# Cross-attention weights transposed by DMA instead of TensorE, in a quantised transformer layer on one core

## The chip, the cores and the metric

The kernel runs on one core of a Trainium2 chip. The metric is device time in microseconds (us). A core has TensorE (PE in the profile; PEld is its weight load), VectorE (DVE), ScalarE (ACT), GpSimd (POOL) and SyncE (SP), which here only issues DMAs. Each engine runs its own instructions in order and waits for the others through semaphores; DMAs move data in the background.

## The reference, cut to what matters

For 32 batches of 100 rows, `x` (32, 100, 256) is normalised and attends to a context of 361 rows with 16 heads of width 64; then comes a feed-forward layer whose operands are quantised.

```python
Qh = einsum('btd,hdk->bhtk', layernorm(x), WQ)
Kh = einsum('btd,hdk->bhtk', ctx, WK)
Vh = einsum('btd,hdv->bhtv', ctx, WV)
logits = einsum('bhtk,bhsk->bhts', Qh, Kh) / 8 + mask * -1e9
attn = softmax(logits)
A = einsum('bhts,bhsv->bhtv', attn, Vh)      # heads side by side
x = x + A @ WO
x = x + qlinear(gelu(qlinear(layernorm(x), W1, b1)), W2, b2)
```

The change concerns `attn`. Scores come out with the 100 query rows on partitions and the 361 context rows in the free dimension; the product with `Vh` sums over context rows, so it needs `attn` with the context rows on partitions. Every one of the 512 matrices (32 batches, 16 heads) of 100x361 float32 has to be transposed.

## The kernel before, in words

Batches are handled one after the other, 16 heads as 8 pairs (`NHP`); a pair's two heads lie in the lower and the upper 64 partitions of queries (`qbuf`) and keys (`kT`). Batch 0 and batch 31 are cut into three steps of 2, 2, 4 and 4, 2, 2 pairs; the other 30 batches are one step each ("whole", `turns` in the code). Four batches make a group: queries, and the product with `WO`, are computed for a group at once.

The main loop (from L616) issues for a whole batch, on PE in just this order, since PE is kept to the order of the source by `manual_schedule` while the other engines are left to a planner:

- For each of the 8 pairs, in turn: `weights_T` (L363) of the batch before: 12 PE transposes (2 heads, 3 chunks of 128 context rows, 2 halves of 50 queries; L373) into two PSUM banks, and two copies to `pT` (L385, on ACT but for the first, which is on DVE); then the scores of the pair (L423), into two PSUM banks. DVE adds the mask, writes the scores to the SBUF buffer `pb` (16 slots, one a head) and finds each row's extreme (L434); ACT then makes the exponentials and their sums (L404), DVE the reciprocals of the sums and the division (L443, L449).
- `attend` of the batch before (L468): `pT` times the values, copied to `aT` by ACT (L475).
- `v_part` (L287), the batch's values, copied by DVE (L294).
- A group's work, in one of the four batches each: `project_T` (`py`, L505), `project_back` (`po`, L519) with the residual on DVE and a store by POOL (L529 to L546, L135), `ln1_T` (`ptx`, L336), `q_part` (`pq`, L348).
- `k_part` of the next batch (`pk`, L256): 8 pairs, copied to `kT` by ACT (L263).

The 50-query halves lie at partitions 0 and 64 (`RH`), so scores take 114 partitions (`TP`). All PSUM tiles of attention share a ring of 8 banks (`bank`, L191), handed out in the order of the source. Contexts are loaded by SP (L197) into three buffers, two or three batches ahead. Steps of quantising the feed-forward weights (`quantize_weight`, L559) are put in two to a batch. The feed-forward part (from L680) follows when attention has ended.

The two functions that do the transposing and hand it on, as they are before:

```python
for h in range(2):
    for c in range(NSC):
        for k in range(2):
            ks = slice(k * RH, k * RH + TH)
            nc.tensor.transpose(
                pts[k][:SC, (h * NSC + c) * TH : (h * NSC + c + 1) * TH],
                pb[ks, h0 + h, c * SC : (c + 1) * SC],
                ident[ks, ks],
            )
```

Of the kernel before, what the change touches and what calls it, by code (L numbers as in the profile page):

```python
# [8 lines left out]
F32 = mybir.dt.float32  # L9
BF16 = mybir.dt.bfloat16  # L10
I16 = mybir.dt.int16
# [10 lines left out]
BIG = 3.4e38  # L22
# [5 lines left out]
def kernel(  # L28
# [34 lines left out]

    TH, RH = T // 2, P // 2
    TP = RH + TH

# [72 lines left out]
    def normalize(b, after, engine=nc.vector):  # L139

        xb = xg[b // G][:, b % G, :]
        i = engine.tensor_scalar(
            xb, xb, mv2[:, b, 0:1], rstd2[:, b : b + 1], ALU.subtract, ALU.mult
        )
        follow(i, after)
# [13 lines left out]
    with ExitStack() as att:  # L159
# [14 lines left out]
        maskt = wpool.tile([TP, S], F32, tag="maskt", name="maskt")  # L174
        nc.gpsimd.memset(maskt, 0.0)
# [3 lines left out]
        pb = wpool.tile([TP, 2 * NHP, SP], F32, tag="p", name="p")  # L179
        for t in cbuf:  # L180
# [4 lines left out]
            wpool.tile([P, PAIRS, G, 2, RH], F32, tag=f"q{q}", name=f"q{q}") for q in range(NQ)  # L185
        ]
        for t in qbuf:
            for j in range(G):
                nc.gpsimd.memset(t[:, :, j, 0, TH:], 0.0)
# [31 lines left out]
        for k in range(2):  # L221
            nc.scalar.dma_start(
                out=maskt[k * RH : k * RH + TH], in_=mask[k * TH : (k + 1) * TH]
            )
        load_w(nc.sync, wqt, 0, wq)
# [16 lines left out]
        steps = []  # L242
        for b in range(B):
            first = 0
            for n in parts.get(b, (NHP,)):
                steps.append((b, first, n))
                first += n
# [93 lines left out]
        def q_part(g, q):  # L341

            if g >= NG:
                return
            for pair in range(PAIRS):
                pq = bank(f"pq{g}_{q}_{pair}")
                for dc in range(NDC):
                    nc.tensor.matmul(  # L348
                        pq[:, :GT],
                        wqt[q][:, dc, pair * P : (pair + 1) * P],  # L350
                        xnTs[g][:, dc, :],
                        start=(dc == 0),
                        stop=(dc == NDC - 1),
                    )
                nc.vector.tensor_scalar(
                    qbuf[q][:, pair, :, :, :TH],
                    pq[:, :GT].rearrange("p (j k t) -> p j k t", j=G, k=2),
                    -1.0 / DK**0.5, None, ALU.mult,
                )
# [3 lines left out]
        def weights_T(i, pair, on_vector):  # L363
# [5 lines left out]
# [3 lines that stand above are left out]
                        ks = slice(k * RH, k * RH + TH)  # L372
                        nc.tensor.transpose(  # L373
                            pts[k][:SC, (h * NSC + c) * TH : (h * NSC + c + 1) * TH],
                            pb[ks, h0 + h, c * SC : (c + 1) * SC],
                            ident[ks, ks],
                        )
            pT = pTs[i, pair] = p1.tile(
                [SC, 2 * NSC, 2, TH], F32, tag=f"pT{pair}", name=f"pT{i}_{pair}"
            )  # L380
            copies = []
            for k in range(2):
                src = pts[k][:SC, : 2 * NSC * TH].rearrange("p (c t) -> p c t", t=TH)
                copy = nc.vector.tensor_copy if k == 0 and on_vector else nc.scalar.copy
                copies.append(copy(pT[:, :, k, :], src))  # L385
            return copies

        def scores(i):

            b, first, n = steps[i]
            g, j = b // G, b % G
            _, p0, before = steps[i - 1] if i else (0, 0, 0)
            turns = n == NHP
            heads = range(2 * first, 2 * (first + n))
            rsum = small.tile([TP, 2 * NHP], F32, tag="rsum", name=f"rsum{i}")
            r = small.tile([TP, 2 * NHP], F32, tag="r", name=f"r{i}")
            ms = {}

            def exponentials(heads):
                for h in heads:
                    s = pb[:, h, :S]
                    done = nc.scalar.activation(  # L404
                        s, s, AF.Exp, bias=ms[h], scale=-1.0, accum_out=rsum[:, h : h + 1]
                    )
                    if turns:
                        follow(done, copied)

            if not turns:  # L410
                for pair in range(p0, p0 + before):
                    weights_T(i - 1, pair, True)
            for pairs in ([q] for q in range(first, first + n)) if turns else (
                range(q, q + PAIRS) for q in range(first, first + n, PAIRS)
            ):
                if turns and pairs[0] < before:
                    copied = weights_T(i - 1, p0 + pairs[0], pairs[0] == 0)[1]
                pss = {}
                four = range(2 * pairs[0], 2 * pairs[-1] + 2)
                for h in four:  # L420
                    pair, k = divmod(h, 2)
                    pss[h] = bank(f"sc{i}_{h}")
                    nc.tensor.matmul(  # L423
                        pss[h][:TP, :S],
                        qbuf[pair // PAIRS][
                            k * DK : (k + 1) * DK, pair % PAIRS, j, :, :
                        ].rearrange("p k t -> p (k t)")[:, :TP],
                        kT[k * DK : (k + 1) * DK, pair, :],
                        start=True,
                        stop=True,  # L430
                    )
                for h in four:
                    ms[h] = small.tile([TP, 1], F32, tag=f"m{h}", name=f"m{i}_{h}", bufs=1)
                    found = nc.vector.tensor_tensor_reduce(  # L434
                        pb[:, h, :S], pss[h][:TP, :S], maskt, 1.0, BIG, ALU.add, ALU.min, ms[h]
                    )
                if not turns:
                    exponentials(four)
            if turns:
                exponentials(heads)  # L440
            at_once = 1 if i == len(steps) - 1 else 4
            for h0 in heads[::at_once]:
                last = nc.vector.reciprocal(  # L443
                    r[:, h0 : h0 + at_once], rsum[:, h0 : h0 + at_once]
                )
                follow(last, found)
                for h in range(h0, h0 + at_once):
                    s = pb[:, h, :S]
                    nc.vector.tensor_scalar(s, s, r[:, h : h + 1], None, ALU.mult)  # L449
            return last  # L450

        def attend(i, pairs=None):
# [8 lines left out]
            for p0 in range(first, first + n, HP):  # L461
                m = min(HP, n)
                av = bank(f"av{i}_{p0}")
                for pair in range(p0, p0 + m):
                    for c in range(NSC):
                        for k in range(2):
# [4 lines left out]
                                pTs[i, pair][:, k * NSC + c, :, :].rearrange("p k t -> p (k t)"),  # L471
# [87 lines left out]
        def quantize_weight(src, rows, dst, name, n, after):  # L559
# [16 lines left out]
            if n == NWP:  # L576
                al = small.tile([P, NWP], F32, tag="aal", name=f"aal{name}")
                nc.gpsimd.partition_all_reduce(al, am, P, bass_isa.ReduceOp.max)
                sw = const.tile([P, 1], F32, tag=f"sw{name}", name=f"sw{name}")
                rw = small.tile([P, 1], F32, tag="rw", name=f"rw{name}")  # L580
                nc.vector.tensor_reduce(sw, al, AX.X, ALU.max)
# [3 lines left out]
            if n > NWP:  # L585
# [3 lines left out]
                nc.vector.tensor_scalar(  # L589
# [9 lines left out]
        for b in range(G):  # L599
            stats1(b)  # L600
        nc.vector.tensor_scalar(maskt, maskt, 1e9, None, ALU.mult)
# [10 lines left out]


        todo = [(w, n) for w in ("1", "2") for n in range(2 * NWP + 1)]
        weights = {"1": (w1T, NDC, w1qt), "2": (w2T, NFC, w2qt)}
        for i, (b, first, n) in enumerate(steps):  # L616
            g, j = b // G, b % G
            begun = [h for h in range(2) if first <= h * HP < first + n]
            ended = [h for h in range(2) if first < (h + 1) * HP <= first + n]
            last = scores(i)  # L620
            if i >= 1:
                attend(i - 1)
# [13 lines left out]
            for h in ended:  # L636
                k = 2 * j + h
                if k < G:
                    stats1((g + 1) * G + k, last)
                if k == 2 * (G - 2) + 1:  # L640
                    ln1(g + 1, first_copied)
                if g >= 1 and 2 <= k < 2 + G:
                    project_back(g - 1, k - 2)
                if k == 2 * (G - 2) + 1:
                    ln1_T(g + 1)
                if j == G - 1:
                    for q in range(2):
                        q_part(g + 1, 2 * h + q)
                if g >= 1 and k == 1:
                    for dc in range(NDC):  # L650
                        project_T(g - 1, dc)
                if h == 1 and b + NCB < B:
                    load_ctx(b + NCB)
# [5 lines left out]
            if i >= 3:  # L659
                for w, p in todo[:2]:  # L660
                    quantize_weight(*weights[w], w, p, last)
                del todo[:2]
# [343 lines left out]
```

## Time and profile before

| what | before |
|---|---|
| median of 3 runs | 1337.61 us (1337.61 to 1337.65) |
| the profiled execution | 1336.85 us |
| its span, first to last instruction | 1335.1 us |
| busy: PE, PEld, DVE, ACT, POOL | 1306.2, 807.5, 774.2, 695.8, 113.6 us |
| instructions: PE, DVE, ACT, POOL | 10062, 2404, 1927, 198 |
| granted TensorE clock | 0.995 |
| DMA | 33.02 MB, mean 25 GB/s |

The span is that of one execution, whose own time is 1.75 us longer. A group row of the profile gives busy time (with overlaps of pipelined instructions counted once) and the mean duration of one instruction; the chain of waits follows the end of the kernel back to its start, each piece once, so its pieces add up.

### The profile page before, as it was taken

To read this page: it belongs to the slowest core of one execution; us is meant where nothing else is said; L and a number is where in the kernel's file an instruction comes from. 1 tells how busy PE (TensorE), PEld (TensorE's weight loads), DVE (VectorE), ACT (ScalarE), POOL (GpSimd) and SP (SyncE) were. 2 spreads that over 40 slices of the span, in tenths; PEclk is the share of its full clock that TensorE was granted. 3 is DMA by queue.
4 is the path that set the end of the run, shared out by engine and by line. 5 is a ranking of instruction groups with operands and counts; after the bars stand their busy time and mean duration, and the time that the engine had idled before them with its cause. 6 is when DMAs were issued, how large, how long until landed. Compare 5 with 4: busy or idle time off the path is not lost.

```text
span 1335.1 us, 25493 instructions
## 1 busy us (share of the span) xinstructions
PE 1306.2 (98%) x10062; PEld 807.5 (60%) x10064; DVE 774.2 (58%) x2404; ACT 695.8 (52%) x1927; POOL 113.6 (9%) x198
## 2 busy tenths in 40 slices
PE   9999999999999999999999999999999999999858
PEld 4666556666566566666566666665666665666426
DVE  4666446664366554664366653664556643576897
ACT  2555345565355455562456453553455543554875
POOL 1000000200011000110011000110001100110260
PEclk9999999999999999999999999999999999999999
DMA  8010001000000000000000000000000000000112
GB/s 247 28 44 13 12 12 44 20 17 1 12 19 18 12 12 1 19 19 12 13 18 19 12 2 12 18 18 12 12 2 18 19 13 12 11 11 4 49 54 99
DMA packets 24864, 33.02 MB, mean 25 GB/s; under 512 B 1828, under 2 KB 22792, under 8 KB 24744
## 3 DMA queue, kind: packets, MB, share of 16 engines
q1 hardware_dynamic: 21776, 24.81, 6.3%
q0 software_dynamic: 2144, 5.38, 1.3%
q8 instruction: 79, 1.29, 0.4%
q10 hardware_dynamic: 824, 1.19, 0.3%
q14 instruction: 41, 0.34, 0.1%
HBM read 24.82 MB, written 6.55 MB: 24 GB/s over the span
## 4 chain that ended last, share of the span: by engine, by line
PE 94%; POOL 2%; issue 2%; ACT 1%; DVE 1%; POOLq 0%; DVEq 0%
PE pv L287 25%; PE pk L256 23%; PE sc L423 13%; PE av L468 10%; PE pt L373 7%; PE pq L348 6%; PE py L505 6%; PE pf L950 2%; PE po L489 1%; ACT h L860 1%; POOL r L797 1%; POOL r L798 1%; PE po L519 0%; PE ptx L336 0%; PE ph L852 0%
## 5 line engine op out<-in xcount | busy, mean ns | idle before, releaser
L287 PE MATMUL pv<-wvt,c 128*128 128x512 f32 x768 | 338.3, 596 | 0.0
L256 PE MATMUL pk<-c,wkt 128*128 128x361 f32 x1016 | 314.2, 467 | 0.0
L263 ACT COPY kT<-pk 128x361 f32<-128x361 f32 x254 | 116.8, 460 | 366.6 <-PE pk L256 366.6
L404 ACT ACTIVATE p<-p,m 114x361 f32<-114x361 f32 x512 | 297.4, 592 | 7.8 <-DVE m L434 7.8
L256 PEld LDWEIGHTS pk<-c,wkt 128*128 128x128 f32 x1016 | 191.9, 190 | 113.2 <-issue 1.0
L434 DVE CUSTOM_DVE_ANT_0 p<-sc,maskt 114x361 f32<-114x361 f32 x512 | 252.2, 533 | 11.9 <-PE sc L423 6.9
L287 PEld LDWEIGHTS pv<-wvt,c 128*128 128x128 f32 x768 | 143.3, 190 | 172.1 <-issue 161.9
L385 DVE COPY pT<-pt 128x300 f32<-128x300 f32 x50 | 22.3, 468 | 351.6 <-PE pt L373 351.6
L423 PE MATMUL sc<-kT,q 64*114 64x361 f32 x1024 | 208.5, 490 | 0.0
L385 ACT COPY pT<-pt 128x300 f32<-128x300 f32 x462 | 168.7, 413 | 74.1 <-PE pt L373 71.4
L373 PEld LDWEIGHTS pt<-ident,p 50*128 50x128 f32 x3072 | 131.1, 139 | 78.1 <-issue 51.5
L449 DVE TENSOR_SCALAR p<-p,r 114x361 f32<-114x361 f32 x512 | 173.5, 403 | 2.6
L294 DVE COPY v<-pv 128x512 f32<-128x512 f32 x192 | 129.4, 680 | 28.6 <-PE pv L287 28.3
L468 PEld LDWEIGHTS av<-pT,v 128*64 128x64 f32 x3072 | 132.8, 137 | 18.5 <-ACT pT L385 15.0
L468 PE MATMUL av<-pT,v 128*64 128x100 f32 x3072 | 140.0, 250 | 0.0
L373 PE MATMUL pt<-ident,p 50*128 50x50 f32 x3072 | 133.5, 221 | 0.3 <-DVE p L449 0.3
L135 POOL TENSOR_TENSOR xb<-x,b2a 100x256 f32<-100x256 f32 x32 | 23.4, 732 | 900.4 <-DVE rmax L529 891.2
L404 ACT ACTIVATION_READ_ACCUMULATOR p<-p,m 114x1 f32 x512 | 99.7, 195 | 0.0
L348 PE MATMUL pq<-xnT,wqt 128*128 128x400 f32 x256 | 87.9, 500 | 0.2 <-ACT xnT L339 0.2
L423 PEld LDWEIGHTS sc<-kT,q 64*114 64x114 f32 x1024 | 76.8, 184 | 4.3 <-issue 0.6
L505 PE MATMUL py<-aT,wot 128*128 128x400 f32 x224 | 76.4, 499 | 0.0
L443 DVE RECIPROCAL r<-rsum 114x4 f32<-114x4 f32 (+1 forms) x131 | 22.8, 175 | 90.2 <-ACT p L404 89.9
(131 smaller groups left out, 730.7 us busy)
## 6 DMA issues: line engine op xcount, KB each, us to landing
c<-in_ctxT_dram SPq DMA_DIRECT2D x31, 361.0 KB, 3.1
x<-in_x_dram SPq DMA_DIRECT2D x8, 400.0 KB
xb<-xb POOLq DMA_DIRECT2D x32, 100.0 KB, 2.1
x<-xb SPq DMA_DIRECT2D x5, 384.0 KB, 3.0
out_dram<-ot SPq DMA_DIRECT2D x3, 384.0 KB, 2.5
wqt<-in_wq_dram SPq DMA_DIRECT2D x4, 256.0 KB
wot<-in_wo_dram SPq DMA_DIRECT2D x1, 1024.0 KB, 8.9
w<-in_w1T_dram POOLq DMA_DIRECT2D x1, 1024.0 KB, 5.4
```

The source lines that it names most:

```text
L256: nc.tensor.matmul(pk[:, :S], wkt[q][:, dc, col * P : (col + 1) * P], c[:, dc, :S], start=(dc == 0), stop=(dc == NDC - 1),)
L287: nc.tensor.matmul(pv[:SC, :], c[:, dc, s * SC : (s + 1) * SC], wvt[h][:, dc, :], start=(dc == 0), stop=(dc == NDC - 1),)
L294: return nc.vector.tensor_copy(vs[b, h][:, s, :], pv[:SC, :])
L348: nc.tensor.matmul(pq[:, :GT], wqt[q][:, dc, pair * P : (pair + 1) * P], xnTs[g][:, dc, :], start=(dc == 0), stop=(dc == NDC - 1),)
L373: nc.tensor.transpose(pts[k][:SC, (h * NSC + c) * TH : (h * NSC + c + 1) * TH], pb[ks, h0 + h, c * SC : (c + 1) * SC], ident[ks, ks],)
L385: copies.append(copy(pT[:, :, k, :], src))
L404: done = nc.scalar.activation(s, s, AF.Exp, bias=ms[h], scale=-1.0, accum_out=rsum[:, h : h + 1])
L423: nc.tensor.matmul(pss[h][:TP, :S], qbuf[pair // PAIRS][k * DK : (k + 1) * DK, pair % PAIRS, j, :, :].rearrange("p k t -> p (k t)")[:, :TP ...
L434: found = nc.vector.tensor_tensor_reduce(pb[:, h, :S], pss[h][:TP, :S], maskt, 1.0, BIG, ALU.add, ALU.min, ms[h])
L449: nc.vector.tensor_scalar(s, s, r[:, h : h + 1], None, ALU.mult)
L468: nc.tensor.matmul(av[k * DK : (k + 1) * DK, (pair - p0) * T : (pair - p0 + 1) * T], vs[b, pair // HP][:, c, h * DK : (h + 1) * DK], pTs[i ...
L505: nc.tensor.matmul(py[:, :GT], wot[:, c, dc * P : (dc + 1) * P], aT[:, c, :, :].rearrange("p j t -> p (j t)"), start=(c == 0), stop=(c == ...
```

## The change

In the 30 whole batches the weights are no longer transposed on PE. The float32 weights are seen as pairs of 16-bit halves. For a pair of heads, POOL copies the 2 x 384 float32 of each query row into one of two buffers `apart`, with the low halves and the high halves of each chunk of 128 in separate rows of 128 (`send`: two copies of 100 x 768 int16). SP then issues one DMA transpose of that buffer (112 x 1536 int16, 336 KB) into one of three buffers `xT`. ACT copies `xT` into `pT`, putting the halves together again (`join`: one copy of 128 x 1200 int16 a pair).

The order of a whole batch is written anew (`whole_batch`), in four quarters of two pairs (four heads): scores of the quarter, then its part of the next batch's keys; `attend` of the batch before in the second quarter; half the values in the third and in the fourth. `pb` has 8 slots instead of 16, so a slot comes round after two quarters. DVE, ACT and POOL, like PE, keep the order of the source within whole batches. Scores of whole batches take 100 partitions instead of 114; the 114-partition mask stays, as `maskh`, for batches 0 and 31, which go on being transposed by PE. Some small work moves (`quantize_weight` in more steps, `load_ctx` to the first quarter of the next batch, the end of a batch's loop body to `rest`).

```diff
+    TR = -(-T // 16) * 16
...
-        pb = wpool.tile([TP, 2 * NHP, SP], F32, tag="p", name="p")
+        NB = 4 * PAIRS
+        pb = wpool.tile([TP, NB, SP], F32, tag="p", name="p")
...
+        apart = [
+            wpool.tile([TR, 2 * NSC * 2 * SC], I16, tag=f"apart{k}", name=f"apart{k}")
+            for k in range(2)
+        ]
...
+        def products(i, pairs):
+            b = steps[i][0]
+            n = TP if halved(b) else T
+            pss = {}
+            for h in range(2 * pairs[0], 2 * pairs[-1] + 2):
+                pair, k = divmod(h, 2)
+                pss[h] = bank(f"sc{i}_{h}")[:n, :S]
+                nc.tensor.matmul(
+                    pss[h],
+                    qbuf[pair // PAIRS][k * DK : (k + 1) * DK, pair % PAIRS, b % G, :n],
+                    kT[k * DK : (k + 1) * DK, pair, :],
+                    start=True,
+                    stop=True,
+                )
+            return pss
+        def minima(i, pss):
+            for h, ps in pss.items():
+                n = ps.shape[0]
+                ms[h] = small.tile([TP, 1], F32, tag=f"m{h}", name=f"m{i}_{h}", bufs=1)
+                done = nc.vector.tensor_tensor_reduce(
+                    pb[:n, h % NB, :S], ps, maskh if halved(steps[i][0]) else maskt, 1.0, BIG,
+                    ALU.add, ALU.min, ms[h][:n],
+                )
+            return done
...
+        xTs, NX = {}, 3
+        def send(i, q):
+            n = NSC * 2 * SC
+            for pair in range(q * PAIRS, (q + 1) * PAIRS):
+                src = apart[pair % 2]
+                for k in range(2):
+                    nc.gpsimd.tensor_copy(
+                        src[:T, k * n : (k + 1) * n].rearrange("t (c l s) -> t c l s", c=NSC, l=2),
+                        pb[:T, (2 * pair + k) % NB, :].bitcast(I16).rearrange(
+                            "t (c s l) -> t c l s", c=NSC, l=2
+                        ),
+                    )
+                xT = xTs[i, pair] = p1.tile(
+                    [SC, 2 * NSC * 2, TR], I16, tag="xT", name=f"xT{i}_{pair}", bufs=NX
+                )
+                nc.sync.dma_start_transpose(out=xT, in_=src)
+        def join(i, q):
+            for pair in range(q * PAIRS, (q + 1) * PAIRS):
+                pT = pTs[i, pair] = p1.tile(
+                    [SC, 2 * NSC, T], F32, tag=f"pT{pair}", name=f"pT{i}_{pair}"
+                )
+                nc.scalar.copy(
+                    pT.bitcast(I16).rearrange("s c (t l) -> s c t l", l=2),
+                    xTs[i, pair][:, :, :T].rearrange("s (c l) t -> s c t l", l=2),
+                )
...
+        def whole_batch(i):
+            b = steps[i][0]
+            g, j = b // G, b % G
+            late = []
...
+            for q in range(NQ):
+                heads = range(2 * PAIRS * q, 2 * PAIRS * (q + 1))
+                minima(i, products(i, range(q * PAIRS, (q + 1) * PAIRS)))
+                if q == 1:
+                    divide(i, range(2 * PAIRS))
+                    send(i, 0)
+                exponentials(i, heads)
+                if q == 0 and b - 1 + NCB < B:
+                    load_ctx(b - 1 + NCB)
+                n = steps[i + 1][2] // NQ
+                for pair in range(q * n, (q + 1) * n):
+                    k_part(i + 1, pair)
+                if q == 0 and whole(i - 1):
+                    join(i - 1, NQ - 1)
+                if q == 1:
+                    attend(i - 1)
+                    last = divide(i, heads)
+                    send(i, 1)
...
+                if q >= 2:
+                    join(i, q - 2)
+                    for c in range(NSC):
+                        v_part(b, q - 2, c)
+                        if c == 0:
+                            divide(i, heads)
+                            send(i, q)
...
+            rest(i, range(2), None)
+            join(i, NQ - 2)
...
+        engines = {getattr(mybir.EngineType, e) for e in ("DVE", "Activation", "Pool")}
+        first_whole = steps.index((1, 0, NHP))
+        for i in range(first_whole):
+            part_of_batch(i)
+        with tc.manual_schedule(engines=engines):
+            for i in range(first_whole, first_whole + B - 2):
+                whole_batch(i)
+        for i in range(first_whole + B - 2, len(steps)):
+            part_of_batch(i)
```

`divide` and `exponentials` are the reciprocals with the division, and the exponentials, of the old `scores`, as functions of their own; `part_of_batch` is the old loop body for the steps of batches 0 and 31.

## The prediction

> **What bounds the kernel now.** I read the page's busy times and its chain of waits first.
>
> ```profile
> PE 1306.2 (98%) x10062; PEld 807.5 (60%) x10064; DVE 774.2 (58%) x2404; ACT 695.8 (52%) x1927; POOL 113.6 (9%) x198
> ...
> PE 94%; POOL 2%; issue 2%; ACT 1%; DVE 1%; POOLq 0%; DVEq 0%
> PE pv L287 25%; PE pk L256 23%; PE sc L423 13%; PE av L468 10%; PE pt L373 7%; PE pq L348 6%; PE py L505 6%; PE pf L950 2%; PE po L489 1%; ACT h L860 1%; POOL r L797 1%; POOL r L798 1%; PE po L519 0%; PE ptx L336 0%; PE ph L852 0%
> ```
>
> PE sets the end; the transposes (pt) are 7% of the chain. Pipelined matmuls overlap in their group row, so I take their price from the chain in order of time, one batch of it (pieces: start, duration, what):
>
> ```profile
> 668.88 0.51 PE pt L373 x12
> 669.38 0.66 PE sc L423 x4
> 670.04 0.36 PE pt L373 x12
> 670.40 0.66 PE sc L423 x4
> ...
> 677.18 4.27 PE av L468 x96
> 681.46 10.50 PE pv L287 x24
> 691.95 0.44 PE po L519 x4
> 692.39 9.71 PE pk L256 x32
> 702.10 0.51 PE pt L373 x12
> ```
>
> The pieces follow without a gap: 33.22 us from pt to pt. The next batches take 33.94, 43.53 (with pq, 10.75) and 43.53 (with py, 10.75): 154.2 a group of four, two light batches and two heavy.
>
> **Removed from PE.** A whole batch has 8 pieces of 12 transposes, one of 0.51 and seven of 0.36: 3.03 us, 30 times: 90.9 us. As a check, 7% of 1335.1 is 93.5, and 30/32 of it 87.6. Scores and keys keep their number of instructions and 361 moving columns; only their order changes. So a batch's floor becomes 30.2, 30.9, 40.5 or 40.5 us, and the profiled execution's 1336.85 would become 1246.0, on the scale of the median (0.76 higher) 1246.7.
>
> **Moved to the other engines**, with these rows of the groups by shape (busy us, mean ns of one, idle before and its releaser):
>
> ```profile
> L404 ACT ACTIVATE p<-p,m 114x361 f32<-114x361 f32 x512 | 297.4, 592 | 7.8 <-DVE m L434 7.8
> ...
> L752 POOL TENSOR_SCALAR xq<-ix,hix 100x1024 bf16<-100x1024 int16 x6 | 6.7, 1109 | 16.4 <-ACT ix L738 9.0 <-DVE ix L736 7.4
> ...
> L937 ACT ACTIVATE ih<-h,rsh 128x1024 int16<-128x1024 f32 x4 | 4.3, 1134 | 0.0
> ```
>
> and, for DMAs, these (last column: median us from issue to landing):
>
> ```profile
> c<-in_ctxT_dram SPq DMA_DIRECT2D x31, 361.0 KB, 3.1
> ...
> xb<-xb POOLq DMA_DIRECT2D x32, 100.0 KB, 2.1
> ```
>
> *ACT.* A batch has 16 exponentials at 592 + 195 ns, 8 copies of kT at 460, 2 of aT at 484: 17.2 us. It loses 15 copies of pT (413 each, 6.2 us) and gains 8 joins of 1200 16-bit elements. From 1134 ns for 1024 elements and 1565 for 1536, one is J = 1.28 us; the bf16 copy of xqT (851 for 800) gives 1.2. 8 J = 10.2, so ACT does 27.5 of at least 30.2 us: it fits, closely. No row reads elements so far apart: J could double (20.5; ACT 37.7, which would be 2.2 a group over the old 154.2, 1354 in all), and the lower end is 1.1 (the PSUM copies' slope).
>
> *POOL.* 16 copies of 768 int16. C: the nearest row, int16 in and 16 bits out on 100 partitions, is 1109 ns for 1024; with 243 for a one-element instruction that is 0.85 ns an element, 0.89 for 768. The dearest one-input row on 100 partitions, 1241 ns for 256 (normalisation), would give 3.2, the 128x800 float32 row (2216) 2.1. At 3.2 loop 1 (below) is 43.6 us a batch, 1496 in all. I take C = 1.1, a little above the nearest row since the source steps by two. 17.6 us a batch beside up to 5.5 of POOL's own: hidden.
>
> *DMA.* D is the time from a finished copy to landed halves. No row transposes. A plain load of 361 KB lands in 3.1 us, the shortest row is 2.1, the longest 8.9 (1024 KB). I take D = 4.5, above the row of its size for the unknown transposing. The Trainium skill (DMA: Bandwidth & Descriptors, Latency and other measured facts) gives a transpose 261 GB/s; an estimate by that page is 1.3 us for 336 KB, with its fixed 2.0 us D = 3.3, and the total would be 1250.
>
> *DVE.* 16 minima at 615 ns, 16 divisions at 403, 4 reciprocals at 175, 6 value copies at 680: 21.1 us, about 2.5 of residual and statistics, as before less one pT copy. Hidden; if it were not, each microsecond over a light batch's floor would cost 15 us in all.
>
> *At nothing:* one more mask load and scaling, fewer clears of qbuf, clears of apart, the split weight steps: beside PE's first 17 us or single instructions of 0.3 to 0.7 us on engines with room. The context load behind the transposes on SP has a whole batch before its first use.
>
> **What the waits make of it.** With sources in order I follow a light batch from PE's first score (t = 0): scores of the second quarter at 3.8, attend 7.5 to 11.8, third scores 11.8, fourth 20.8, end 30.2.
>
> - ACT: first exponentials from about 1, kT to 5.1, then join of the last two pairs of the batch before to 7.7. attend reaches those pairs near 11.2: 3.5 us spare. Second exponentials end at 10.9.
> - DVE: division of the second quarter 10.9 to 12.7, behind it minima of the third 12.7 to 15.2; a value bank that PE asks for at 19 needs them. Spare again.
> - The turn-round has two loops. **Loop 1** is apart: a buffer is free when its DMA has landed, so two pairs cost 2C + D, a batch 4(2C + D): 26.8. **Loop 2** is the three xT: pair 5's DMA waits for the join of pair 2, pair 7's copy for pair 5's DMA (same apart buffer), and pair 7's join stands on ACT ahead of the second exponentials, behind which come division (1.8), minimum (0.7), third exponentials, joins 0 and 1, fourth exponentials and join 2 again: 2D + 2C + 3(3.15) + 2(0.9) + 4J + 2.5, about 2D + 21.1. With D = 4.5 that is 30.1, just under 30.2.
>
> So PE is not held up while D is below 4.5. At D = 5 loop 2 is 31.1: 0.9 + 0.2 a group, 7.5 groups, 8 us. As my D stands at the edge, I add half of that, 4 us, and 3 us once where batch 31 begins: there only 2.6 us of scores stand ahead of attend, whose last join ends near 9. 1246.7 + 4 + 3 = **1254 us**.
>
> **The rivals.**
>
> 1. *The loops run a little slow* (D 5.2 to 6.5, or J near 1.8). At D = 6 loop 2 is 33.1: 2.9 + 2.2 a group, 38 us, 1292 in all; range 1275 to 1335. For it: ACT has under 3 us of room, and its waits in order are lost. Against: heavy batches have 10 us of slack each.
> 2. *Slower: the turn-round of the two apart buffers becomes the period.* Four batches took 154.2; two heavy at 40.5 leave 36.6 for a light one, so loop 1 decides from 2C + D = 9.15, or D = 7 at my C (at D = 3.1, C = 3). At D = 7.5 it is 38.8, +4.4 a group, 1371; at the longest landing row, 8.9, 44.4, +23.4 a group, 1513. For it: nothing here shows a transpose, and each passes 1344 row pieces of 256 bytes. Against: the plain load of that size needs 3.1.
> 3. *POOL and DVE hold each other up.* DVE's division reads and writes SBUF at 0.52 ns an element ((745 - 403) over (1024 - 361)), against 1.48 for the minimum from PSUM: a double rate. If POOL stands still meanwhile, two divisions of a quarter fall into loop 2, 0.8 us each at most: 31.7 at D = 4.5, +2.3 a group, 17 us, 1264 without the half term. Against: POOL's sum xb stays at 713 to 749 ns over 24 batches. The Trainium skill (GPSIMD Engine Reference, Key points) says POOL shares its SBUF interfaces with DVE and contends with its 2-port mode; by that rule it comes out as in this rival, and no run here shows it.
> 4. *No change:* loop 1 lands near 36.6 by chance.
>
> **How the numbers follow.** Forecast 0.42 (1241 to 1275: the 91 us may be 5 more or less, as chain pieces border on each other); rival 1 0.24; rival 2 0.21; rival 3 0.10 (1255 to 1275); rival 4 0.03. A measurement can tell about 0.2%, 2.7 us. Faster: 0.42 + 0.24 + 0.10 = 0.76; same 0.03; slower 0.21. The range goes from 1241 to 1365, which leaves out the greater part of rival 2 (0.16) and a little below.
>
> **What would show it.** Right: no L373 in whole batches, light batches at 30.2 to 31 us, POOL copies near 1.1 us, joins near 1.28, transposes landing within 4.5 us, PE still over 93% of the chain. Wrong: ACT waiting for xT at join, POOL waiting for a DMA ahead of its copies, or DVE ahead of minima for POOL, with PE idle before attend or before scores; or SP so long at one transpose that eight fill a batch.

## The result, and the profile after

| what | before | after |
|---|---|---|
| median | 1337.63 us (4 runs) | 1285.52 us (4 runs, 1282.22 to 1286.68) |
| ratio | | 0.9605, 95% interval 0.9587 to 0.9623 |
| profiled execution, its span | 1336.85, 1335.1 | 1286.68, 1284.4 |
| PE's first scores; end of attention (first warm-up matmul after it), us from the start | 21.4; 1244.1 | 23.9; 1193.7 |

The change is worth 52 us. The forecast was 1254, with 1275 to 1335 as the first rival. In the profiled executions attention ends 50.4 us earlier, not 90.9; the feed-forward part takes as long as before. So some 40 us are missing inside attention.

The page's busy times and chain of waits, after:

```profile
PE 1251.3 (97%) x7182; PEld 704.0 (55%) x7184; DVE 864.9 (67%) x2403; ACT 818.9 (64%) x1721; POOL 515.0 (40%) x672
...
PE 86%; DVE 5%; issue 3%; POOL 3%; ACT 3%; DMA 0%; POOLq 0%; DVEq 0%; ACTq 0%
PE pk L280 24%; PE pv L311 23%; PE sc L435 13%; PE av L540 10%; PE pq L372 7%; PE py L577 6%; PE pf L1097 2%; ACT h L1007 1%; DVE p L478 1%; DVE v L318 1%; PE po L561 1%; POOL r L944 1%; POOL r L945 1%; POOL apart L503 0%; DMA xT<-apart 0%
```

PE lost 2880 transposes and still bounds the kernel; 8% of the chain has gone from PE to the other rows, half of it to DVE. The rows of the new work, from the groups by shape (busy, mean ns, idle before):

```profile
L503 POOL COPY apart<-p 100x768 int16<-100x768 int16 x480 | 397.7, 863 | 609.6 <-DVE p L478 405.7 <-DMA xT<-apart 133.8 <-DVE m L449 20.8
...
L519 ACT COPY pT<-xT 128x1200 int16<-128x1200 int16 x240 | 309.9, 1336 | 35.2 <-DMA xT<-apart 35.1
...
L478 DVE TENSOR_SCALAR p<-p,r 100x361 f32<-100x361 f32 x480 | 253.6, 591 | 4.2
```

The prediction's C, one of POOL's copies, is 0.86 us (taken as 1.1), and J, one join on ACT, 1.34 (1.28). The division, whose code is as before, takes 591 ns on average instead of 403. D, from a finished copy to landed halves, is read from single instructions: a pair's copies end at 625.0 us into the span but its DMA starts at 625.98, when a join has freed an xT; it has landed by 629.55, when POOL's waiting copy starts: 3.6 us, of which SP holds 1.36 for the issue. Of two pairs sent close behind each other the first took 4.8 (issue at 617.04, waiting copy at 621.85).

The chain in order of time for a heavy batch (start, duration, what):

```profile
607.75 1.39 PE sc L435 x8
609.14 2.62 PE pk L280 x8
611.77 1.39 PE sc L435 x8
613.16 2.62 PE pk L280 x8
615.78 4.27 PE av L540 x96
620.05 1.39 PE sc L435 x8
621.45 2.62 PE pk L280 x8
624.07 5.15 PE pv L311 x12
...
638.39 10.75 PE py L577 x32
649.14 1.39 PE sc L435 x8
```

The lines left out are the fourth quarter, 1.39, 2.62 and 5.15 again. No gap, and yet 41.38 to 41.39 us from first scores to first scores instead of 43.53 - 3.03 = 40.50. Scores are 4 x 1.39 = 5.56 (before 8 x 0.66 = 5.28), keys 4 x 2.62 = 10.48 (9.71), values 10.30 (10.50): together 0.85 more a batch, with the same matmuls. This is most of what is missing; the experiments ask what it is.

### The profile page after: what moved, and what is told of

It is laid out like the page before. It is cut to its first block, busy times and chain, and to the rows that moved or that the text cites. A ratio compares the mean times of both kernels' runs of the same rounds, so it can differ in the third digit from the quotient of the medians.

```text
span 1284.4 us, 21400 instructions
## 1 busy us (share of the span) xinstructions
PE 1251.3 (97%) x7182; PEld 704.0 (55%) x7184; DVE 864.9 (67%) x2403; ACT 818.9 (64%) x1721; POOL 515.0 (40%) x672
## 3 DMA queue, kind: packets, MB, share of 16 engines
q10 hardware_dynamic: 934, 1.34, 0.4%
## 4 chain that ended last, share of the span: by engine, by line
PE 86%; DVE 5%; issue 3%; POOL 3%; ACT 3%; DMA 0%; POOLq 0%; DVEq 0%; ACTq 0%
PE pk L280 24%; PE pv L311 23%; PE sc L435 13%; PE av L540 10%; PE pq L372 7%; PE py L577 6%; PE pf L1097 2%; ACT h L1007 1%; DVE p L478 1%; DVE v L318 1%; PE po L561 1%; POOL r L944 1%; POOL r L945 1%; POOL apart L503 0%; DMA xT<-apart 0%
## 5 line engine op out<-in xcount | busy, mean ns | idle before, releaser
L503 POOL COPY apart<-p 100x768 int16<-100x768 int16 x480 | 397.7, 863 | 609.6 <-DVE p L478 405.7
L463 ACT ACTIVATE p<-p,m 100x361 f32<-100x361 f32 (+1 forms) x512 | 299.1, 588 | 253.3 <-DVE m L449 252.7
L519 ACT COPY pT<-xT 128x1200 int16<-128x1200 int16 x240 | 309.9, 1336 | 35.2 <-DMA xT<-apart 35.1
L449 DVE CUSTOM_DVE_ANT_0 p<-sc,maskt 100x361 f32<-100x361 f32 x480 | 227.2, 529 | 131.7 <-PE sc L435 119.8
L478 DVE TENSOR_SCALAR p<-p,r 100x361 f32<-100x361 f32 (+1 forms) x512 | 264.5, 579 | 4.4
L435 PE MATMUL sc<-kT,q 64*100 64x361 f32 (+1 forms) x1024 | 191.8, 484 | 0.4
L435 PEld LDWEIGHTS sc<-kT,q 64*100 64x100 f32 (+1 forms) x1024 | 78.2, 163 | 92.4 <-issue 16.8
L463 ACT ACTIVATION_READ_ACCUMULATOR p<-p,m 100x1 f32 (+1 forms) x512 | 96.4, 188 | 0.0
L372 PEld LDWEIGHTS pq<-xnT,wqt 128*128 128x128 f32 x256 | 48.4, 190 | 38.8 <-issue 3.3
L577 PEld LDWEIGHTS py<-aT,wot 128*128 128x128 f32 x224 | 42.6, 190 | 34.0 <-issue 3.3
```

The costliest lines, as they stand in the source:

```text
L372: nc.tensor.matmul(pq[:, :GT], wqt[q][:, dc, pair * P : (pair + 1) * P], xnTs[g][:, dc, :], start=(dc == 0), stop=(dc == NDC - 1),)
L435: nc.tensor.matmul(pss[h], qbuf[pair // PAIRS][k * DK : (k + 1) * DK, pair % PAIRS, b % G, :n], kT[k * DK : (k + 1) * DK, pair, :], start= ...
L449: done = nc.vector.tensor_tensor_reduce(pb[:n, h % NB, :S], ps, maskh if halved(steps[i][0]) else maskt, 1.0, BIG, ALU.add, ALU.min, ms[h] ...
L463: nc.scalar.activation(s, s, AF.Exp, bias=ms[h][:n], scale=-1.0, accum_out=sums[i][0][:n, h : h + 1])
L478: nc.vector.tensor_scalar(s, s, r[:n, h : h + 1], None, ALU.mult)
L503: nc.gpsimd.tensor_copy(src[:T, k * n : (k + 1) * n].rearrange("t (c l s) -> t c l s", c=NSC, l=2), pb[:T, (2 * pair + k) % NB, :].bitcast ...
```

## The experiments

The theories: **A**, PE itself loses time wherever scores and other matmuls follow one another in the new order. **B**, TensorE is slowed by the new traffic (DMA, POOL) or the clock. **C**, the waits among DVE, POOL and ACT are the main loss. Four of the kernels below were run once (keys among the scores before, no copies, one buffer apart, all 128 rows), the others four times.

### Keys among the scores in the kernel before

```diff
+                elif pairs[0] % 2 and steps[i + 1][2] == NHP:
+                    for pair in (pairs[0] - 1, pairs[0]):
+                        k_part(i + 1, pair)
```

(at the end of each pair's turn in `scores`; the block of eight at the end of the batch is left out)

> The kernel before, with one part of the change alone: in whole batches the next batch's keys come in four lots of two pairs among the scores, instead of in one block of eight at the end; transposes stay on TensorE, no DMA transposes, no 16-bit copies. Theory A (the order itself costs: at each passage between the 64-row score matmuls and the 128-row key matmuls PE loses 0.1 to 0.2 us, so that keys took 10.49 us a batch after the change instead of 9.71 and scores 5.56 instead of 5.28): the lots of keys take about 2.6 us for 8 instead of 2.43, and the time rises by 0.6 to 1.2 us in each of 29 batches, 1355 to 1372. Theory B (PE's pieces grew because DMA transposes, POOL's copies or the clock slow TensorE's reads): lots at 2.43, time within 4 us of 1337.6.

1372.8 us against 1337.1 in the same comparison: 35.7 more, with no DMA transpose and no copy on POOL. Its chain in order of time:

```profile
604.00 0.51 PE pt L373 x12
...
605.17 0.36 PE pt L373 x12
605.53 0.66 PE sc L423 x4
606.19 2.62 PE pk L256 x8
608.82 0.51 PE pt L373 x12
```

The lot of eight key matmuls costs 2.62 here too, and each lot makes the next transposes 0.51 instead of 0.36: 4 x 0.19 and 3 x 0.15 are 1.2 a batch, 29 batches, 35. Theory B falls for this part of the loss; A holds.

### Keys in two lots, in one, in three

```diff
-                n = steps[i + 1][2] // NQ
-                for pair in range(q * n, (q + 1) * n):
-                    k_part(i + 1, pair)
+                n = steps[i + 1][2] // 2
+                if q % 2:
+                    for pair in range(q // 2 * n, (q // 2 + 1) * n):
+                        k_part(i + 1, pair)
```

> The changed kernel, but with the next batch's keys in two lots of four pairs (after the scores of the second and of the fourth quarter) instead of four lots of two. Theory A: two of four passages to and fro are gone, 0.35 to 0.45 us a batch, 30 batches, so 1272 to 1275 if no new wait comes of it; lots of 16 key matmuls take about 5.0 us. Theory B, or the waits as the main loss: 1283 to 1290, or slower, as PE now reaches the second scores 2.6 us earlier.

> The changed kernel with all eight pairs of the next batch's keys in one lot, after the scores of the fourth quarter. Theory A by itself gives 0.6 to 0.7 us a batch less, 1265. But then attend follows the second scores at once, 2.8 us into the batch, and its last two pairs stand on joins that end 7 to 9 us in; PE stalls by 1 to 3 us a batch, and ACT's eight copies of kT stand behind the fourth exponentials: 1285 to 1330. If the interleaving only costs and hides nothing, 1265; if it buys time for the turn-round, over 1285.

Two lots: 1293.5, ratio to before 0.9669 (0.9653 to 0.9685); one lot: 1330.4, 0.9957 (0.9942 to 0.9972). PE's pieces shrink as A says (the 32 key matmuls take 10.48 in four lots, 10.10 in two, 9.90 in one), but the whole is slower. With two lots the chain has a heavy batch with 41.0 us, and then a light one:

```profile
654.24 2.61 PE sc L435 x16
656.85 5.05 PE pk L280 x16
...
667.56 5.35 PE pv L311 x12
...
679.36 1.73 PE pv L311 x4
...
681.11 0.69 DVE v L318
...
681.92 2.50 DVE p L478 x4
684.42 1.19 DVE v L318 x2
...
688.37 0.86 PE sc L435 x2
```

16 scores in one piece are 2.61, less than twice 1.39; values behind scores are 5.35, behind keys 5.15. So it is the passage from scores to anything and back that costs, whatever comes. But here PE waits from 681 on: the path goes over DVE, which has four slowed divisions (2.50), value copies, statistics and the residual ahead of the minima that free the next bank. The two light batches of a group come to 30.7 and 33.7 to 35.4 us, against 31.07 and 32.5. In the change's own order the keys between first and second scores fill that time: the interleaving costs some 26 us, and with one lot, without it, the kernel is 45 slower.

Three lots (two pairs in the first and in the second quarter, four in the fourth), with the two edits of the section on the single gap besides:

> As e7, with the next batch's keys in three lots: two pairs in the first and the second quarter, none in the third, four in the fourth. Theory A prices a passage from scores to any 128-row matmul, not to keys alone: the values that now follow the third scores pay the same 0.2 us as e2's did (5.35 instead of 5.15), so nothing is saved on PE, and heavy batches stay at 41.3 to 41.4 us; time within 4 us of e7, or slower by waits. If the passage costs only with keys, heavy batches fall to 41.1 and the time by 6 to 8 us.

1282.99, against 1281.27 for the same kernel with four lots. Heavy batches 41.38 to 41.39, the values behind the third scores 5.35: nothing saved on PE, as A said.

### Scores over all 128 rows

```diff
-                    qbuf[pair // PAIRS][k * DK : (k + 1) * DK, pair % PAIRS, b % G, :n],
-                    kT[k * DK : (k + 1) * DK, pair, :],
+                    qbuf[pair // PAIRS][:, pair % PAIRS, b % G, :n],
+                    kT[:, pair, :],
```

> The changed kernel with score matmuls over all 128 partitions of queries and keys instead of 64, so that a head's scores become the sum of both heads' of its pair (that changes the computation) and no matmul of attention uses 64 rows, but the order is the same. If the passage costs because PE changes between 64-row and 128-row operation, it is gone: lots of 8 keys take 2.43 us (2.62), values after keys 5.15; 8 score matmuls no longer run two abreast and take 8 x 0.304 = 2.43 us (1.39), so the time rises by 4 x 1.04 - 4 x 0.19 = 3.4 us in 30 batches, about 1385. If the passage costs because any other operands or PSUM banks follow, lots of keys stay at 2.62, scores take 2.6, and the time is about 1425.

```profile
663.23 2.43 PE sc L435 x8
665.66 2.43 PE pk L280 x8
668.09 2.43 PE sc L435 x8
670.51 2.43 PE pk L280 x8
672.94 4.27 PE av L540 x96
677.21 2.60 PE sc L435 x8
679.81 2.43 PE pk L280 x8
```

With the order unchanged and 64-row matmuls gone, keys are at 2.43 exactly, and scores pay 0.17 only behind attend, whose matmuls use 64 columns of the array. The loss is that of changing between a divided and an undivided array: 0.17 us on the way in (2 x 1.39 - 2.61) and 0.2 on the way out (2.62 - 2.43, 5.35 - 5.15). The Trainium skill (TensorEngine Tiling (Array Packing), Key Properties) has the rule: changing the tiling mode drains TensorE. The trace agrees in that each change priced here costs 0.15 to 0.2 us; the drain itself no run shows. A group of four batches takes 159.7 us instead of 146.4, 3.3 a batch as expected. The time, 1397.3, is 12 over the forecast, mostly because that counted the 30 whole batches alone: batches 0 and 31 have such scores too and take 4.9 and 4.6 us more than in the change.

### Without POOL's copies

```diff
-                for k in range(2):
-                    nc.gpsimd.tensor_copy(
...
-            nc.gpsimd.memset(t[T // 32 * 32 :], 0.0)
+            nc.gpsimd.memset(t, 0.0)
```

> The changed kernel without POOL's 480 copies: the DMA transposes send whole apart buffers that are cleared once, so the weights that reach the values are left out of the computation; everything else runs. Theory A (PE's order is 26 us of the 39 that are missing, waits a few): DVE's division falls from 0.59 back to 0.40 us, light batches lose their wait of some 0.8 us a group, time 1272 to 1281, PE's lots of keys stay at 2.62. Rival C (DVE and POOL holding each other up is the main loss): 1245 to 1262.

1277.32. Its row of the division, from the groups by shape:

```profile
L478 DVE TENSOR_SCALAR p<-p,r 100x361 f32<-100x361 f32 x480 | 164.0, 406 | 4.2
```

So the copies are what lengthens the division, 406 to 591 ns; but all that they cost the kernel is 8 us. Most of that is the single gap of the next section: 6.6 us, and it is not there in this run. The second light batch of a group takes 32.14 us instead of 32.52. Keys stay at 2.62. Theory C falls as the main loss.

### The single gap, and the start

After the change one batch, and no other, is 6.6 us longer (47.98 instead of 41.38 between first scores). The chain there leads through a transpose:

```profile
265.11 1.36 DVE p L478 x4
...
269.64 1.61 POOL apart L503 x2
271.27 5.32 DMA xT<-apart
...
276.72 2.42 ACT p L463 x8
279.13 0.35 ACT kT L287
279.53 6.00 PE av L540 x96
```

POOL issues the 1 MB load of the second weight at 260.86 (1.01 us), in a light batch; it has landed at 268.34. Two edits, the second kernel having both:

```diff
+            for w in ("1", "2") for n in (*((None,) * 4 if w == "2" else ()), 0, None, *range(1, 2 * NWP + 1))
...
         q_part(0, 0)
+        for t in apart:
+            nc.gpsimd.memset(t[T // 32 * 32 :], 0.0)
```

> The changed kernel with the load of the second feed-forward weight (1 MB, issued by POOL) two batches later, in a heavy batch instead of a light one. Theory D (the single 6.6 us gap near 275 us is that load: POOL's issue of 1.0 us stands ahead of its copies, and transposes land late while 1 MB goes through the same DMA engines; the 10.75 us of group work at the end of a heavy batch takes that up): the gap is gone, the median 5 to 7 us lower, 1278 to 1281. Otherwise it moves with the load or stays: 1283 to 1288.

> As e6, and the two clears of apart on POOL come after the first queries instead of before them. If the clears (1.4 and 1.6 us on POOL ahead of the first reciprocal roots) are what moved PE's first scores from 21.4 to 23.9 us, these come back to 21.0 to 22.0, and the time is 2 to 3 us below e6, 1275 to 1279. If the start is late for another reason, the time is that of e6.

1281.37 and 1281.27 (ratios to before 0.9581, 0.9566 to 0.9597, and 0.9577, 0.9563 to 0.9592). Moving the load takes 4.2 us off and most of the gap: 1.1 to 1.7 us stay in that batch. The transpose of 5.32 us is not the load's doing: it was issued after the load had landed, and with the load moved the chain has one like it in the same batch:

```profile
271.75 5.50 DMA xT<-apart
```

What the load delays is the work ahead of it. The DMA packets of the transpose issued at 264.30 begin 3.0 us after their issue and end after 4.7, where the medians of all 240 transposes are 1.17 and 2.99. Why the later transpose is slow in both runs is left open.

Moving the clears gives nothing: in that run PE's first scores come at 23.5 us, because PE's first matmuls wait for a weight (its chain has 6.75 us of that DMA). Why the start is 2 us later than before is left open.

### One buffer apart

```diff
-                src = apart[pair % 2]
+                src = apart[0]
```

> The changed kernel with one buffer apart instead of two, so that copies and DMA of a pair follow one another for all 8 pairs of a batch. Loop 1 of the prediction becomes 8(2C + D): with C = 0.85 and a lone transpose of D = 3.6 us, 42.4 us a batch, in light and heavy batches alike; from 41.4 + 41.4 + 31.8 + 31.8 that is 23 a group of four, 7.5 groups: 1455, range 1430 to 1490. If the copies and DMAs were hidden with much room, or D were 2.5, loop 1 would be 33.6 and the time about 1315.

1549.9, past the range. A pair does take what loop 1 of the prediction says. POOL, in order of time (idle before, and for what):

```profile
648.21 1.60 POOL L503 COPY apart<-p 100x768 int16<-100x768 int16 x2 [4.08 <-DMA xT<-apart]
...
653.42 1.60 POOL L503 COPY apart<-p 100x768 int16<-100x768 int16 x2 [3.61 <-DMA xT<-apart]
...
658.64 1.60 POOL L503 COPY apart<-p 100x768 int16<-100x768 int16 x2 [3.62 <-DMA xT<-apart]
...
663.84 1.60 POOL L503 COPY apart<-p 100x768 int16<-100x768 int16 x2 [3.61 <-DMA xT<-apart]
```

1.60 + 3.61 = 5.21 a pair, 41.7 for eight; the prediction's C and D are confirmed. But a batch costs more than the loop: POOL's other work comes between two pairs (665.41 to 672.03 in this stretch, 3 us more than the landing alone). What makes up the rest is not shown, and the granted clock of this one run was 0.939 against 0.993. A loop's length is a lower bound.

### Four xT; the residual out of DVE's way

```diff
-        xTs, NX = {}, 3
+        xTs, NX = {}, 4
```

```diff
+                put = deferred.append if whole(i) and whole(i + 1) else lambda f: f()
...
+                    put(lambda k=k: stats1((g + 1) * G + k, last))
...
+                    put(lambda k=k: project_back(g - 1, k - 2))
...
                 minima(i, products(i, range(q * PAIRS, (q + 1) * PAIRS)))
+                if q == 0:
+                    while deferred:
+                        deferred.pop(0)()
```

> As e7, with four buffers xT instead of three (room comes from fewer buffers of small tiles). Loop 2 of the prediction then waits for a join one pair earlier. With the measured C = 0.83, D = 3.6 and J = 1.34 loop 2 is about 28 us, under the floor of a light batch, so it should not bind: light batches stay at 31.1 to 32.5, time within 2.7 us of e7's 1281.3. If the three buffers were what holds light batches up: 1274 to 1278.

> As e7, with keys in two lots as in e2, and with the residual and the statistics (DVE, 3 to 4 us in a light batch) moved from the end of a batch to behind the first minima of the next. Theory: in e2 one passage a batch was saved (heavy batches 41.0), but PE stood in light batches for a bank, because DVE came to the next minima only after four slowed divisions, two value copies, and the residual. With the residual out of that queue light batches fall from 33 to about 31: 1268 to 1275. If the slowed divisions alone hold DVE up: light batches 32 to 33, 1283 to 1292.

> As e7 (keys in four lots), with residual and statistics moved behind the first minima of the next batch. The light batches' remaining wait is 0.4 to 0.8 us a group: 1276 to 1281 if it goes, within 2.7 us of e7 if it does not. PE's lots stay at 2.62 and 1.39, heavy batches at 41.4.

1280.37 (0.957, 0.9555 to 0.9584) with four xT, where 1281.27 is the time with three: loop 2 did not bind. Residual later: 1278.55 (0.9552, 0.9536 to 0.9568) with two lots, 1277.57 (0.9547, 0.9533 to 0.9561) with four. With two lots heavy batches are mostly 41.0 and the first light batch 30.26, but the second is 31.7 to 34.5 and the next heavy one 42.1 to 42.2: the saving is given back, and the 1268 to 1275 expected do not come. The chain of that second light batch goes through a transpose (4.65), a division of 2.74 and the group's normalisation (3.32); which of them takes the saving is not shown. With four lots the light batches fall to 30.64 and 31.71: the wait at their end goes, 3.7 us in all against 1281.27. From the kernel with two lots this last one cannot be told apart.

## Why the prediction was right in sign and 31 us off

**Right.** PE is the bound and the transposes were on it: 3.03 us a batch are gone. C (0.86), J (1.34) and D (3.6, 4.8 in a pair of transposes) lie near the values taken; the turn-round fits in a batch, and four xT gain nothing. Slower (rival 2) needed D = 7 and did not come. That the time lies in the stated range is luck: the range reaches so far because slower rivals were counted in, and the cause of most of the loss stands in none of them.

**The step that failed**: "Scores and keys keep their number of instructions and 361 moving columns; only their order changes." The order is not free. Moving the keys from one block to four lots adds passages between 64-row and 128-row matmuls. The prediction put this at nothing; it measured 41.38 - 40.50 = 0.88 us a batch, some 26 us in all. The row was there: in the profile before, the first transposes behind the keys are 0.51, the others 0.36, and the prediction used both without asking why.

The rest, from the intervals between first scores in the profiled executions: the two light batches of a group take 31.07 + 32.52 = 63.6, where their pieces make 31.07 + 31.79 = 62.9 (31.79 is 31.07 and the 0.72 of `ptx`): 0.7 in each of six groups, 4.4 us. The single gap is 6.6, the start 2.5, batch 0 1.0. With 25.5 (0.88 in 29 batches) that is 40 of the 40.5 missing. The allowance of 4 us for the light batches' waits had the right size, but the prediction gave it to loop 2; in the trace the chain leaves PE for DVE:

```profile
674.63 1.73 PE pv L311 x4
...
677.19 2.50 DVE p L478 x4
679.69 1.19 DVE v L318 x2
...
685.07 1.30 PE sc L435 x4
```

Moving the residual takes this wait away, four xT do not. The 3 us for the end were not needed.

**Rival 1** gave the range that held (1275 to 1335) for the wrong reason: neither loop was slow. **Rival 3** had the right place and the wrong loser. POOL's copies stay at 0.83 to 0.94; it is DVE that waits. DVE and POOL of the changed kernel in order of time:

```profile
614.72 0.72 DVE L478 TENSOR_SCALAR p<-p,r 100x361 f32<-100x361 f32 x2
615.36 0.97 DVE L478 TENSOR_SCALAR p<-p,r 100x361 f32<-100x361 f32 x1
616.25 0.96 DVE L478 TENSOR_SCALAR p<-p,r 100x361 f32<-100x361 f32 x1
```

```profile
615.25 0.88 POOL L503 COPY apart<-p 100x768 int16<-100x768 int16 x1 [14.64 <-DVE p L478]
616.08 0.94 POOL L503 COPY apart<-p 100x768 int16<-100x768 int16 x1
```

Two divisions, begun beside no copy, take 0.72 together. The third and the fourth begin inside a copy and end 0.2 us after that copy does. The Trainium skill (SBUF — State Buffer, Who interferes with whom) says that of a DVE instruction in 2-port mode and a POOL one the second to issue is blocked until the first has ended: this trace agrees, 0.97 beside a copy and 0.41 alone; that the division runs in that mode no run shows. It cost 8 us at most, the copies' whole price.

Two figures of the working stand on another base than their neighbours. C = 3.2 gives 7.5 x 20.2 more than 1337.6, 1489; 1496 has the two allowances (4 and 3 us) in it, which the 1371 and 1513 of rival 2 have not. Rival 3's 1264 leaves out both allowances, not the 4 us alone. Nothing rests on them.

## What to carry to other kernels

On an engine that is full, price a new order by its passages, not only by its instructions: look in the trace for the same instruction at two prices (0.51 and 0.36, 9.71 for 32 and 2.62 for 8) and count how often the new order has the dear one. Before dissolving an interleaving to save them, ask what it hides: one lot had the cheapest keys and the slowest kernel of the three. And a large background load is best put where PE has a long stretch of work that waits for nobody: here that was worth 4 us.

## What the runs showed of the hardware that was not expected

- A change between 64-row and 128-row matmuls costs PE 0.17 to 0.2 us each way; with 128 rows throughout it is gone (keys 2.43 instead of 2.62).
- A DMA transpose of 112x1536 16-bit elements (336 KB) from SBUF to SBUF holds SP for 1.36 us and lands after 3.6; the first of two close together 4.8. Its packets begin 1.17 us after the issue and end after 2.99 (medians of 240).
- Setting 16-bit halves apart costs POOL 0.83 us for 768 elements a row, and joining them ACT 1.34 for 1200 read with a stride: close to what contiguous rows gave (0.89 and 1.28 in the prediction's sums).
